# Expert lists' remainders in quarters of 32 slots, paired loads of weights, and no conditional block

## The chip, the cores and the metric

The kernel runs on one core of a Trainium2 chip. The metric is the device time of one execution in microseconds (us); several executions were timed and one was profiled. TensorE (PE, and PEld for its loads of stationary operands), VectorE (DVE), ScalarE (ACT), GpSimd (POOL) and SyncE (SP, which here issues the large loads) work side by side and wait for each other by semaphores. All data is float32.

## The reference

```python
x = x + xattn(ctx_1024, layernorm(x), fside, ...)       # x: 4 x 1024 x 256, context of 77, 16 heads
h = layernorm(x)                                        # 4096 tokens of 256
probs = softmax(h @ Wr); w, idx = top_k(probs, 2)       # 9 experts, each token goes to two of them
cw[t, idx] = w / sum(w)
hidden = silu(h @ Wg[e]) * (h @ Wu[e])                  # 256 -> 704, for each expert e
x = x + einsum(hidden, Wd[e], cw)                       # 704 -> 256, weighted by cw
```

Each of the 4096 tokens is computed by only its two experts, so there are 8192 entries in nine lists of unknown length.

## The kernel before

**Two stages.** In the first, attention is computed in 32 sub-blocks of 128 tokens and each token is put on the lists of its two experts (an entry is the token's number and its weight). The second runs the experts over the lists. Lists lie in memory (`list_d`); normed tokens lie in `y_d`; the output already holds the residual and the experts' results are added to it there.

**Blocks.** The second stage is a sequence of blocks, written out when the kernel is built, whose experts and list places come from tables computed on the chip (`early_blocks`, `late_blocks`, both on VectorE). A *pair* block takes 256 slots of one expert, a *single* block 128. Six pairs ("early") are placed before all lists are complete; the rest after. There are 26 pairs in all (NPAIR). The lists' remainders go in singles: eleven with 128 slots of one expert ("one") and five with two halves of 64 slots, each half of its own expert ("flex"). The order is pair, single, pair, single and so on, with five pairs at the end. The fifth flex block is the *rare* one: its weights are loaded and its rounds of adding are issued in every execution, but its computation stands in `tc.If(count > 2 * (FLEX - RARE))` (L1679) and runs only where a ninth half is needed. In the profiled execution it did not run.

**One block.** For block j, SP loads the expert's weights (`load`, 2.1 MB: gate and up into `wgu`, down into `wd`; three buffers and four). POOL gathers the block's entries (`tokens`, `ids`) and then the tokens' rows (`inputs`, `yin`, three buffers; two gathers for a pair, one for a single). VectorE turns `yin` into `xT` in 16 steps of 32 lanes (`turning`, L1301). `hidden_pair` (L1328) does six products of 128 features with the weights stationary and the 256 tokens moving; ScalarE and VectorE make `hid` of them. `hidden_one` (L1368) does it for a single, tokens stationary; a flex block issues each product twice, for lanes 0 to 63 with one expert's weights and for lanes 64 to 127 with the other's, and its second weights are in an extra set of buffers (`w2`, `d2`). `hidden_turn` (L1391) transposes a single's result. `down` (L1408) multiplies by `wd`, VectorE weights the result (`co`, L1411).

**Adding.** `adding` (L1443) is an indirect DMA of POOL that adds the 128 rows of `co` to the output. Two rows of one round are never the same token. For a pair, the two halves are declared free of each other. A flex block's two experts may hold the same token, so it is added in two *rounds* (`rounds_of`), each with the lanes of the other half sent out of bounds (`split`, `alone`); a round waits until the round before it, whichever block's, has landed.

**Order.** The order on each engine is written by hand. Iteration j of the loop over blocks does, as each engine sees it: `fetch` (weights of j+2, the second weights of a flex block j+3, rows of j+2, entries of j+4), `hidden` of j with the steps of `turning(j + 1)` laid between VectorE's products (from the third feature group on), `down(j - 1)`, `adding` of j-1, and `hidden_turn(j)` for a single. So POOL's queue holds, in this order: gathers of rows for j+2, gather of entries for j+4, adds of j-1, then the same for the next iteration. While early blocks run, VectorE also makes the late tables, up to twelve small operations between two products (`pump`).

The few lines on which that order rests:

```python
for name, fn, lead in (
    ("weights", weights, LEAD), ("weights_upper", weights_upper, LEAD + 1),
    ("inputs", inputs, LEAD), ("tokens", tokens, LEAD + 2),
):
...
    down(j - 1)
    for r in rounds_of(j - 1):
        adding(*r)
```

Of the kernel before, what the change touches and what calls it, by code (L numbers as in the profile page):

```python
# [8 lines left out]
F32 = mybir.dt.float32  # L9
# [6 lines left out]
P = 128  # L16
# [5 lines left out]
def kernel(  # L22
# [54 lines left out]
    U = P // 2  # L77
    HMAX = (2 * TOK + E * (U - 1)) // U
    NPAIR = -((3 * E - 2 * TOK // U) // 4)
    FLEX = (E + 1) // 2  # L80
    NONE = (HMAX - 4 * NPAIR) // 2 - FLEX

    RARE = 1
    LP = TOK + 3 * P
    ROWS = E * LP + (NONE + 1) * P
# [3 lines left out]
    EARLY = 6  # L89
# [280 lines left out]
    with ExitStack() as kvs:  # L370
# [269 lines left out]
        def wide_iota(name, pattern, shape):  # L640
# [4 lines left out]
        NU = TOK // U  # L645
        steps_i, steps = wide_iota("steps", [[0, E], [U, NU]], [P, E, NU])
        num_i, num = wide_iota("num", [[1, NPAIR], [0, E]], [P, NPAIR, E])
# [3 lines left out]
        lane, lower, upper, lane_half, *nowhere = (  # L651
            tab.tile([P, 1], F32, name=n)
            for n in ("lane", "lo", "up", "lane_half", "nowhere0", "nowhere1")
        )

        def numbers():
            for dst, src in ((steps, steps_i), (num, num_i), (lane, lane_i)):
                nc.vector.tensor_copy(dst, src)
            nc.vector.tensor_scalar(upper, lane, float(U), None, ALU.is_ge)
            nc.vector.tensor_scalar(lower, lane, float(U), None, ALU.is_lt)  # L660
            nc.vector.scalar_tensor_tensor(lane_half, upper, -float(U), lane, ALU.mult, ALU.add)
            for t, half in zip(nowhere, (lower, upper)):
                nc.vector.tensor_scalar(t, half, float(TOK), None, ALU.mult)
# [3 lines left out]
        for name in ("early", "pair", "one", "flex"):  # L667
            sums[name] = [tab.tile([P, PAD + E], F32, name=f"{name}_sum{k}") for k in range(5)]
            for t in sums[name]:
                nc.gpsimd.memset(t[:, :PAD], 0.0)  # L670
# [377 lines left out]
    def place(name, src, n, step, size, shift=None, halves=False):  # L1048

        v = nc.vector
        cur = sums[name][0]
        yield v.tensor_copy(cur[:, PAD:], src)
        for k in range(4):
            nxt = sums[name][k + 1]
            yield v.tensor_tensor(
                nxt[:, PAD:], cur[:, PAD:], cur[:, PAD - (1 << k) : PAD + E - (1 << k)], ALU.add
            )
            cur = nxt  # L1060
        ends = tabs[f"{name}_ends"] = cur[:, PAD:]
        past = tab.tile([P, n, E], F32, name=f"{name}_past")
        yield v.tensor_tensor(
            past, num[:, :n, :], ends.unsqueeze(1).to_broadcast([P, n, E]), ALU.is_ge
# [9 lines left out]
        if shift is None:  # L1074
            yield v.tensor_scalar(weight, src, -float(step), float(size), ALU.mult, ALU.add)
        else:
            yield v.tensor_tensor(weight[:, : E - 1], shift[:, 1:], shift[:, : E - 1], ALU.subtract)
            yield v.tensor_scalar(weight[:, E - 1 :], shift[:, E - 1 :], -1.0, None, ALU.mult)
            yield v.tensor_tensor(weight, weight, src, ALU.subtract)
            yield v.tensor_scalar(weight, weight, float(step), float(size), ALU.mult, ALU.add)  # L1080
# [4 lines left out]
        if shift is None:  # L1085
            yield v.tensor_scalar(at, at, lane[:, 0:1], None, ALU.add)
        else:
            first = tab.tile([P, 1], F32, name=f"{name}_first")
            yield v.scalar_tensor_tensor(
                first, shift[:, 0:1], float(step), lane_half if halves else lane, ALU.mult, ALU.add  # L1090
            )
            yield v.tensor_scalar(at, at, first[:, 0:1], None, ALU.add)
        if halves:
            two = at.rearrange("p (m h) -> p m h", h=2)
            n //= 2
            at = tab.tile([P, n], F32, name=f"{name}_both")
            yield v.tensor_scalar(at, two[:, :, 1], upper, None, ALU.mult)
            yield v.scalar_tensor_tensor(at, two[:, :, 0], lower, at, ALU.mult, ALU.add)
        ai = tab.tile([P, n], I32, name=f"{name}_ai")
        yield v.tensor_copy(ai, at)  # L1100
        tabs[name] = (ei, ai)

# [8 lines left out]
    by_pair, by_unit = "p e (k t) -> p e k t", "p e (k t) -> p e k t"  # L1111

    def early_blocks():

        v = nc.vector
        yield from count_of("early")
        full = row("full")
        ends = steps.rearrange(by_pair, t=4)[:, :, 1:, 0]
        begun = tab.tile(list(ends.shape), F32, name="early_begun")
        yield v.tensor_tensor(  # L1120
            begun, ends, tabs["early_count"].unsqueeze(2).to_broadcast(list(ends.shape)), ALU.is_le
        )
        yield v.tensor_reduce(full, begun, AX.X, ALU.add)
        yield from place("early", full, EARLY, P, LP // 2)
        yield from within("early", full, EARLY, taken)

    def late_blocks():
# [3 lines left out]
        rows = {n: row(n) for n in ("pairs", "used", "units", "alone", "halves")}  # L1131
        pairs, used, units, alone, half = rows.values()

        begun = steps
        yield v.tensor_tensor(
            begun, steps, tabs["late_count"].unsqueeze(2).to_broadcast([P, E, NU]), ALU.is_lt
        )
        yield v.tensor_reduce(pairs, begun.rearrange(by_pair, t=4)[:, :, :, 3], AX.X, ALU.add)
        yield v.tensor_tensor(pairs, pairs, taken, ALU.subtract)
        yield from place("pair", pairs, NPAIR - EARLY, P, LP // 2, taken)  # L1140
        yield from within("pair", pairs, NPAIR - EARLY, used)
        yield v.tensor_tensor(used, used, taken, ALU.add)
        yield v.tensor_scalar(used, used, 2.0, None, ALU.mult)
        yield v.tensor_reduce(units, begun.rearrange(by_unit, t=2)[:, :, :, 1], AX.X, ALU.add)
        yield v.tensor_tensor(units, units, used, ALU.subtract)
        yield from place("one", units, NONE, P, LP, used)
        yield from within("one", units, NONE, alone)
        yield v.tensor_tensor(used, used, alone, ALU.add)
        yield v.tensor_scalar(used, used, 2.0, None, ALU.mult)
        yield v.tensor_reduce(half, begun, AX.X, ALU.add)  # L1150
        yield v.tensor_tensor(half, half, used, ALU.subtract)
        yield from place("flex", half, 2 * FLEX, U, LP, used, halves=True)
        total = tab.tile([P, 1], I32, name="flex_total")
        yield v.tensor_copy(total, tabs["flex_ends"][:, E - 1 : E])
        tabs["flex_total"] = total
# [9 lines left out]
    LAST_PAIRS = NPAIR - EARLY - (NONE + FLEX - RARE)  # L1165
    blocks = [(2, i, "early") for i in range(EARLY)]
    made = {"one": 0, "flex": 0}
    for i in range(NPAIR - EARLY):
        blocks.append((2, i, "pair"))
        if i < NPAIR - EARLY - LAST_PAIRS:  # L1170
            kind = "flex" if i % 3 == 1 and made["flex"] < FLEX - RARE else "one"
            blocks.append((1, made[kind], kind))
            made[kind] += 1
    assert made == {"one": NONE, "flex": FLEX - RARE} and RARE == 1 and LAST_PAIRS > 3
    NBLK = len(blocks)
    blocks.append((1, FLEX - RARE, "flex"))
# [5 lines left out]
    def of(tiles, j):  # L1182

        return tiles[j % len(tiles)] if j < NBLK else late[id(tiles)]

    def open_late():
# [3 lines left out]
        for key, shape, name in (  # L1190
            ("w2", [P, C, 2 * FF], "w2"), ("d2", [P, NF + 1, D], "d2"),
            (id(hids), [P, NF + 1, P], "hid_r"), (id(wds), [P, NF + 1, D], "wd_r"),
            (id(yins), [P, 1, D], "yin_r"),
            ("w", [P, C, 2 * FF], "w_r"), ("xT", [P, C, P], "xT_r"), ("co", [P, 1, D], "co_r"),
            ("hs", [P, FF], "hs_r"),
        ):
            late[key] = pool.tile(shape, F32, name=name)

        for t in (late["d2"], late[id(wds)]):
            nc.gpsimd.memset(t[0:64, NF, :], 0.0)  # L1200
        for key in (id(yins), "co"):
            nc.gpsimd.memset(late[key], 0.0)
# [17 lines left out]

    def weights(j, in_parts=False):

        _, i, kind = blocks[j]
        w = late["w"] if j >= NBLK else pools["wpool"].tile(
            [P, C, 2 * FF], F32, tag="wgu", name=f"wgu{j}"
        )
        two = kind == "flex"
        wgus[j] = (w, late["w2"]) if two else (w,)
        downs[j] = (of(wds, j), late["d2"]) if two else (of(wds, j),)
        at = 2 * i if two else i  # L1230
        parts = load(tabs[kind][0][0:1, at : at + 1], w, downs[j][0])
# [5 lines left out]
    def weights_upper(j):  # L1237

        _, i, kind = blocks[j]
        if kind == "flex":  # L1240
            advance(load(tabs[kind][0][0:1, 2 * i + 1 : 2 * i + 2], late["w2"], late["d2"]))
# [48 lines left out]
    def turned_tile(j):  # L1290
        xT = xTs[j] = late["xT"] if j >= NBLK else pools["spool"].tile(
            [P, C, TS], F32, tag="xT", name=f"xT{j}"
# [433 lines left out]
```

## Time and profile before

| | us |
|---|---|
| nine runs: median (lowest to highest) | 878.71 (876.34 to 884.21) |
| the profiled execution's own time | 876.93 |
| its span, first to last instruction | 874.9 |
| PE busy in the span | 860.8 |
| VectorE, POOL busy | 590.1, 313.9 |
| mean granted TensorE clock | 0.997 |

The profiled execution's time is 2.0 us more than its span. All profile figures below are of this one execution, and times within it count from the span's start. PE's matmul records come in two passes for each float32 product, so a product appears as two records. A timeline line gives start, length, engine, source line, operation, what it writes and reads, the count merged into the line, and in brackets the idle time before it and what ended that. The first stage ends and the late blocks begin at about 442 us.

### The profile page before, as it was taken

The page shows a single profiled execution, that of the slowest core. Times are in us where ns is not written, and L with a number is a line of the kernel's source. Part 1 is how long each engine was busy: PE and PEld are TensorE (multiplying, and loading weights), DVE is VectorE, ACT ScalarE, POOL GpSimd, SP SyncE. Part 2 cuts the span into 40 slices and gives each one's busy share as a digit, 9 for nine tenths or more (in the row PEclk, how much of TensorE's full clock was granted, in tenths as well). Part 3 has the DMA queues.
Part 4 walks back from the last instruction along what each step waited for, and adds up shares of the span by engine and source line. Part 5 has one row for each costly group of instructions (what it writes and reads, how often), then busy time and mean ns, then how long its engine had stood idle before and what let it go on. Part 6 is the DMA issues. An engine that isn't in the chain of part 4 may idle for free. (4 is left out here: it accounts for less than half of the span.)

```text
span 874.9 us, 13839 instructions
## 1 busy us (share of the span) xinstructions
PE 860.8 (98%) x3876; PEld 678.6 (78%) x3876; DVE 590.1 (67%) x1807; ACT 354.4 (41%) x1499; POOL 313.9 (36%) x327
## 2 busy tenths in 40 slices
PE   9999999999999999999999999999999999999996
PEld 6755877778778778988887787777777777778885
DVE  5767779998899987546446566666666666664641
ACT  3868687877878686231211111111111111111110
POOL 3000000413404500657574454445426435444332
PEclk9999999999999999999999999999999999999998
DMA  8026656766576785996697797789779778779722
GB/s 277 2 103 178 177 168 198 195 201 171 176 199 169 215 257 172 283 277 192 153 311 205 219 294 238 231 270 293 235 221 323 218 214 228 223 225 315 211 25 25
DMA packets 133005, 181.22 MB, mean 207 GB/s; under 512 B 26999, under 2 KB 98175, under 8 KB 132800
## 3 DMA queue, kind: packets, MB, share of 16 engines
q1 hardware_dynamic: 115306, 162.90, 61.2%
q0 software_dynamic: 17408, 17.29, 10.2%
q8 instruction: 32, 0.52, 0.2%
q14 instruction: 45, 0.37, 0.1%
q10 hardware_dynamic: 214, 0.13, 0.0%
HBM read 141.54 MB, written 40.41 MB: 208 GB/s over the span
## 5 line engine op out<-in xcount | busy, mean ns | idle before, releaser
L1328 PE MATMUL pg<-xT,wgu 128*128 128x256 f32 x1144 | 252.7, 379 | 1.6 <-DMA wd_r<-in_L_ffn_Wd_dram 1.5
L1328 PEld LDWEIGHTS pg<-xT,wgu 128*128 128x128 f32 x1144 | 215.7, 190 | 31.0 <-issue 1.9
L289 ACT ACTIVATE ex<-psc,mx 128x77 f32<-128x77 f32 x512 | 158.8, 331 | 65.2 <-DVE mx L278 64.9
L1408 PE MATMUL po<-wd,hid 128*128 128x256 f32 (+1 forms) x804 | 180.8, 380 | 0.0
L1408 PEld LDWEIGHTS po<-wd,hid 128*128 128x128 f32 (+1 forms) x804 | 149.2, 187 | 28.0 <-issue 3.7
L1301 DVE STREAM_TRANSPOSE xT<-yin 32x128 f32<-32x128 f32 (+1 forms) x544 | 148.4, 273 | 15.4 <-DMA yin<-y_d,ids 7.2
L1016 POOL DMA_INDIRECT list_d<-r_entry,r_pli x64 | 66.3, 1036 | 252.0 <-DVE r_pli L1003 122.0
L350 PE MATMUL po<-u,aT 128*128 128x265 f32 x640 | 155.6, 398 | 0.0
L1443 POOL DMA_INDIRECT out_dram<-co,ids x63 | 100.4, 1594 | 151.3 <-DVE co L1411 124.0
L350 PEld LDWEIGHTS po<-u,aT 128*128 128x128 f32 x640 | 148.7, 312 | 0.5 <-ACT zT L263 0.4
L274 PE MATMUL psc<-g,zT 128*128 128x462 f32 (+1 forms) x384 | 141.4, 513 | 0.6 <-ACT zT L263 0.5
L1334 ACT ACTIVATE sl<-pg 128x256 f32<-128x256 f32 x130 | 49.8, 384 | 226.0 <-PE pg L1328 201.8
L1335 DVE TENSOR_TENSOR hid<-pg,sl 128x256 f32<-128x256 f32 x130 | 55.0, 424 | 125.0 <-ACT sl L1334 124.3
L274 PEld LDWEIGHTS psc<-g,zT 128*128 128x128 f32 x384 | 72.0, 190 | 57.9 <-issue 44.8
L289 ACT ACTIVATION_READ_ACCUMULATOR ex<-psc,mx 128x1 f32 x512 | 107.8, 211 | 0.0
L1266 POOL DMA_INDIRECT yin<-y_d,ids x67 | 70.6, 1053 | 27.2 <-issue 18.5
L330 DVE STREAM_TRANSPOSE anT<-an 128x1280 f32<-128x1280 f32 x32 | 79.7, 2490 | 0.4 <-DMA a_d<-anT 0.4
L278 DVE TENSOR_REDUCE mx<-psc 128x6 f32<-128x462 f32 (+1 forms) x96 | 53.5, 557 | 21.8 <-PE psc L274 21.8
L1411 DVE TENSOR_SCALAR co<-po,ids 128x256 f32<-128x256 f32 x67 | 32.2, 483 | 49.2 <-PE po L1408 47.4
L311 DVE TENSOR_TENSOR an<-ex,rs 128x1024 f32<-128x1024 f32 x32 | 39.2, 1225 | 1.1
L1396 ACT COPY hid<-ph 128x384 f32<-128x384 f32 x15 | 7.2, 479 | 78.4 <-PE ph L1391 78.4
L1372 ACT ACTIVATE hs<-psg 128x512 f32<-128x512 f32 x15 | 9.0, 597 | 65.3 <-PE psg L1368 65.3
(312 smaller groups left out, 762.3 us busy)
## 6 DMA issues: line engine op xcount, KB each, us to landing
wgu<-in_L_ffn_Wg_dram SPq DMA_DIRECT2D x41, 704.0 KB
wd<-in_L_ffn_Wd_dram SPq DMA_DIRECT2D x41, 640.0 KB
wgu<-in_L_ffn_Wu_dram SPq DMA_DIRECT2D x41, 512.0 KB
a_d<-anT SPq DMA_DIRECT2D x32, 640.0 KB
aT<-a_d SPq DMA_DIRECT2D x128, 160.0 KB
wgu<-in_L_ffn_Wu_dram SPq DMA_DIRECT2D x41, 128.0 KB
x<-in_x_dram SPq DMA_DIRECT2D x8, 512.0 KB
out_dram<-x SPq DMA_DIRECT2D x8, 512.0 KB
```

The costliest lines, as they stand in the source:

```text
L274: nc.tensor.matmul(psc[:, :w], zT[:, c, :], g_sb[i // NS // GPB][:, c, h * J : h * J + w], start=(c == 0), stop=(c == C - 1),)
L278: nc.vector.tensor_reduce(nmx[i][:, h : h + n], psc[:, : n * J].rearrange("p (h j) -> p h j", h=n), AX.X, ALU.max, negate=True,)
L289: nc.scalar.activation(exs[i][:, h + q, :], pscs[k][:, q * J : (q + 1) * J], AF.Exp, bias=nmx[i][:, h + q : h + q + 1], accum_out=sms[i][: ...
L330: nc.vector.transpose(turned.rearrange("p q t k -> p q k t"), an_of[0].rearrange("p (k q t) -> p q k t", q=NQ, t=Q))
L350: nc.tensor.matmul(po[:, :DE], aT[:, :, n], u_sb[b][:, n, :], start=(n == 0), stop=(n == KC - 1))
L1016: i = nc.gpsimd.indirect_dma_start(out=list_d[:, :], out_offset=bass.IndirectOffsetOnAxis(ap=place_i[:, s : s + 1], axis=0), in_=entry.bit ...
L1266: return nc.gpsimd.indirect_dma_start(out=dst, out_offset=None, in_=src, in_offset=bass.IndirectOffsetOnAxis(ap=offsets, axis=0), **kw,)
L1301: yield nc.vector.transpose(xT[q : q + Q].rearrange("p c (h t) -> p h c t", t=P)[:, :nh, :, a : a + Q], of(yins, j)[a : a + Q].rearrange(" ...
L1328: nc.tensor.matmul(pg[:, g, :], w[:, c, at : at + P], xT[:, c, :], start=(c == 0), stop=(c == C - 1),)
L1335: made = nc.vector.tensor_tensor(hid[:, f, :], pg[:, 1, :], sl, ALU.mult)
L1408: nc.tensor.matmul(po[rows, :D], hid[:, f, at], d[:, f, :], start=(f == 0), stop=(f == NF))
L1443: i = nc.gpsimd.indirect_dma_start(out=out_r, out_offset=bass.IndirectOffsetOnAxis(ap=rows_of(j, h, rows), axis=0), in_=cos[j][:, h, :], i ...
```

## The change

The lists' remainders are rounded up to quarters of 32 slots, not to halves of 64. The 26 pairs stay. The singles are now seven "one" blocks, five flex blocks, all computed always, and two "quart" blocks: four quarters of 32 slots, each with its own expert, 14 singles where there were 15 computed ones and the rare one. The `tc.If` and what belonged to it are gone.

Twelve of the pairs form six "quads": two pair blocks of the same expert (`quad`, `quad2`) that share one load of weights. A flex block loads one second set of weights, a quart block three; there are three extra sets (`SETS`), loaded up to five blocks ahead. The last block's weights go to one of these sets.

A quart block issues each product of `hidden_one` and `down` four times, with 32 lanes stationary, and adds in four rounds. The order of the late blocks, numbered from 6 (Q quad and quad2, P pair, O one, F flex, X quart):

```text
QO PF PO QX PO QF PF PO QX PO QF PF, then quad, one, quad2, one, pair
quart blocks: 15 and 27; last block: 39
```

The late tables are made by arithmetic on the counts (`whole`, rounding by adding and subtracting a large number) where a compare of 576 steps was; there are more tables (`quad`, `quart`), and 148 VectorE operations from the late counts to the last table where there were 80. The first two late blocks may be fetched as soon as the quads' table is there (`FETCH`).

```diff
-    U = P // 2
...
-    RARE = 1
+    V = P // 4
...
+    NPAIR, EARLY, QUADS, ONES, FLEX, QUART = 26, 6, 6, 7, 5, 2
+    PARTS = {"early": 1, "quad": 1, "quad2": 1, "pair": 1, "one": 1, "flex": 2, "quart": 4}
...
+    def whole(dst, src, n, up=False):
+        frac = (n - 1) / (2 * n)
+        yield nc.vector.tensor_scalar(dst, src, 1 / n, frac if up else -frac, ALU.mult, ALU.add)
+        yield nc.vector.tensor_scalar(dst, dst, NEAREST, -NEAREST, ALU.add, ALU.add)
...
+        yield from place("quad", doubles, QUADS, 2 * P, LP // 2, begin)
+        yield FETCH
...
+        yield from place("quart", rest, 4 * QUART, V, LP, begin)
...
+    SETS = 3
+    order = "QO PF PO QX PO QF PF PO QX PO QF PF"
...
     def weights(j, in_parts=False):
         _, i, kind = blocks[j]
+        if kind == "quad2":
+            wgus[j], downs[j] = quads.pop(i)
+            return
...
+    def weights_upper(k):
+        def begin(j):
+            _, i, kind = blocks[j]
+            sets = uppers.get(j, ()) if j < LAST else ()
+            if k <= len(sets):
+                at = PARTS[kind] * i + len(sets) - k + 1
+                n = sets[-k]
+                advance(load(tabs[kind][0][0:1, at : at + 1], late["w", n], late["d", n]))
...
     def rounds_of(j):
-        n = 2 if blocks[j][2] == "flex" else 1
-        return [(j, rows) for rows in lanes(range(n))]
+        return [(j, rows) for rows in lanes(range(PARTS[blocks[j][2]]))]
...
+    UPPER = [(f"upper{k}", weights_upper(k), LEAD + k) for k in range(1, SETS + 1)]
...
-        if j == RARE_AT:
-            split(NBLK)
-            with tc.If(count > 2 * (FLEX - RARE)):
-                turn(NBLK)
-                hidden_one(NBLK)
-                hidden_turn(NBLK)
-                down(NBLK)
-            rare = rounds_of(NBLK)
-        elif j > RARE_AT and rare:
-            adding(*rare.pop(0))
```

## The prediction

> **What bounds the kernel now.** I read the page's busy shares first, then PE's timeline block by block, then POOL's timeline and waits.
>
> ```profile
> PE 860.8 (98%) x3876; PEld 678.6 (78%) x3876; DVE 590.1 (67%) x1807; ACT 354.4 (41%) x1499; POOL 313.9 (36%) x327
> ...
> 1.47 4.61 PE L165 MATMUL warm<-u 128*128 128x256 f32 x10 [1.47 <-DVE u L161]
> 6.22 1.56 PE L165 MATMUL warm<-u 128*128 128x256 f32 x6
> ...
> 513.21 9.66 PE L1328 MATMUL pg<-xT,wgu 128*128 128x256 f32 x44
> 522.71 2.75 PE L1408 MATMUL po<-wd,hid 128*128 128x256 f32 x12
> 525.49 1.95 PE L1368 MATMUL psg<-wgu,xT 128*128 128x512 f32 x4
> ...
> 530.29 5.34 PE L1408 MATMUL po<-wd,hid 128*128 128x256 f32 x24
> 535.47 0.82 PE L1391 MATMUL ph<-ident,hs 128*128 128x128 f32 x6
> 536.12 9.66 PE L1328 MATMUL pg<-xT,wgu 128*128 128x256 f32 x44
> ...
> 798.26 2.75 PE L1408 MATMUL po<-wd,hid 128*128 128x256 f32 x12
> 802.55 9.73 PE L1328 MATMUL pg<-xT,wgu 128*128 128x256 f32 x44 [1.53 <-DMA wd_r<-in_L_ffn_Wd_dram]
> ...
> 817.30 9.66 PE L1328 MATMUL pg<-xT,wgu 128*128 128x256 f32 x44
> ```
>
> PE works for 860.8 of 874.9 us, and in the late blocks without a hole but one: 1.53 us at 801, where the conditional stands. So PE's own work sets the end, and whatever stops PE is paid in full. A pair and a single take 536.12 - 513.21 = 22.91 us; a pair alone takes 831.98 - 817.30 = 14.68 (the next pair starts at 831.98); a single is worth 8.23.
>
> POOL is busy for 36%, but its queue is in order and its adds wait:
>
> ```profile
> POOL out_dram L1443 <- DMA out_dram<-co,alone: 25.7, 6, 6.0
> ...
> 503.46 1.62 POOL L1443 DMA_INDIRECT out_dram<-co,alone  x1 [7.37 <-DVE co L1411]
> 511.06 1.59 POOL L1443 DMA_INDIRECT out_dram<-co,alone  x1 [5.98 <-DMA out_dram<-co,alone]
> 512.95 1.07 POOL L1266 DMA_INDIRECT yin<-y_d,ids  x1 [0.30 <-issue]
> 514.33 1.01 POOL L1266 DMA_INDIRECT ids<-list_d,flex_ai  x1 [0.30 <-issue]
> 517.55 1.62 POOL L1443 DMA_INDIRECT out_dram<-co,ids  x1 [2.21 <-DMA out_dram<-co,alone]
> ...
> 837.52 2.71 DMA out_dram<-co_r,alone
> ...
> L740 PE MATMUL pwl<-woT,wc x16: 379/379/403, 41.5 to 42.2; 128*32 128x256 f32 x16
> ```
>
> A flex block's second round starts 7.60 us after its first, released by the first one's landing, and the rows of a later block (L1266) are gathered only behind it. I take this, and not PE, as what decides the change. The line at 837.52 is of the chain of waits: a round with every row out of bounds, 2.71 us from issue to landing on quiet DMAs.
>
> **The change, part by part.** All against the profiled execution: 876.93 us, span 874.9.
>
> *One single less.* 15 computed singles become 14: -8.23 on PE.
>
> *No conditional.* The hole of 1.53 goes. A part of it is the turning of xT, which ended at 801.48 (VectorE's last group, 800.22 + 1.26) where PE was free at 801.0: that is a pair behind a pair with only a single's down between. Two such places come (blocks 14 and 26), each at least 0.5, and their gathers stand behind a flex block's two rounds: 0.5 to 2.0 each, I take 1.0. Together -1.53 + 2.0 = +0.5.
>
> *Flex and quart on PE.* Periods with a flex block take 23.04 and 22.99 against 22.91: 0.2 per flex block. One flex more, and two quarts at 0.2 to 0.4: +0.8 at most. That four products with 32 lanes run side by side is in the L740 line: 16 records of 256 columns start within 0.7 us, where the 128-lane records above take 5.18 / 24 = 0.216 each, so four share a slot. If they ran in turn, a quart's products, 4.7 + 2.6 us, would take three times as much more: +44 us for two.
>
> *Late tables.* 148 operations where there were 80. Before, VectorE was at it from 400 to 420 and 86% busy (18.94 of the 22 us from 399); 68 more at 0.21 are 14 us and end at about 435. From 424 VectorE was nearly idle (3.52 of 16 us from 426), and PE needs the new blocks at 442. Five PSUM banks let PE run 8 us ahead, and by twelve operations (2.5) and one product (0.4) per 1.73 us of PE the lag stays under that. Nothing on the path; if the cover failed, up to 7.
>
> *Weights.* 47 loads become 45. By 7.3 us a load (2.1 MB at the 290 GB/s of busy stretches) and the buffers' releases, each late load lands 12 us or more before its block. Nothing; the extra loads of a quart are spread over three iterations. The first late loads start earlier (DMA share was 0.39 from 400 to 411).
>
> *Four rounds of a quart.* This is where a wait is added. Let T be PE's start on the pair behind quart 15 (block 16). As behind a flex block (490.22 to 503.46) the first round is issued at T + 13.24. Each further round waits for the landing of the one before. Behind the fourth in POOL's queue stand the two gathers of rows for block 19, the entries of 21, the adds of 16. With S the sum of the three spacings, the second gather is issued at T + 13.24 + S + 1.9 + 1.4, and lands 5.1 later (median; 2.7 to 8.4). Then VectorE, whose queue stands at the first of these 16 steps in the middle of block 18, has to do four groups of 1.25 and three products of 0.43: 6.3. So xT of block 19 is there at T + S + 27.9. PE reaches block 19 at T + 12.33 + 10.66 + 9.5 + 2.7 = T + 35.2. PE stands still for S - 7.2 us. Block 31 behind quart 27 is the same.
>
> The spacing: behind rounds with rows, the flex blocks show 7.60, 6.66, 7.59, 6.68, 6.49 and 5.74 (mean 6.8, 64 rows, DMA share 0.85 to 1.0). Behind a round without rows: 3.0 (2.71 + 0.3, quiet) to 4.8 (716.96 to 721.73). The routing of the given inputs fills five of the eight quarters: all four of block 15, one of block 27. A round of 32 rows may land sooner than one of 64: between 3.9 and 6.8, I take 6.1, nearer to the row with rows. Quart 15: S = 18.3, stall 11.1. Quart 27: S = 6.1 + 3.9 + 3.9 = 13.9, stall 6.7. Together +17.8. At the shortest (3.0 all) S = 9.0 and 1.8 each, 3.6 in all; at the longest (7.6, 4.8) 15.6 + 10.0 = 25.6.
>
> In its section on the anatomy of one DMA on the GpSimd path, the Trainium skill's page "DMA: Bandwidth & Descriptors" puts it at about 2.0 us and bytes / 436e3. By it a round of 32 KB would be an estimated 2.1, behind 1.6 of issue and 0.3: spacing 4.0, stalls of 4.8 each and a total of 879, no change. The rows of the trace are far above that beside loads, so I go by them.
>
> *PE after standing.* Records at the start, after idling, are spaced 0.46 (4.61 / 10) and soon 0.22: 2.3 us lost. After the hole of 1.53 nothing (9.73 against 9.66). Between 0 and 2.3 for each stall; idle for 7 to 11 us is nearer to the start: 2.0 each, +4.0. The granted clock reads 1.00 in all of these, so that row doesn't tell it. By Part 1 (the HAM clock gate) of the Trainium skill's page "TensorE: Matmul & The Clock Gate" the array falls to half speed after 3.4 us of idling and needs as long to recover, an estimated 1.7 per stall.
>
> *The end.* Last down, two adds, landing: as before.
>
> Sum: -8.23 + 0.5 + 0.8 + 17.8 + 4.0 = +14.9: 891.8. The nine runs' median lies 1.8 above the profiled execution; I give 892. Bounds: -8.23 - 0.5 + 0.2 + 3.6 = -4.9, 872; and -8.23 + 2.5 + 0.8 + 25.6 + 4.6 = +25.3, 902.
>
> **Rivals.** (1) *The rounds are short enough*: with S under 7.2 there is no stall, and PE's gain stands: -8.23 + 0.5 + 0.8 = -6.9, 870, faster; with some stall 870 to 872. From S = 10.7 at both quarts (spacing 3.6) the gain is gone. For it: a round without rows lands in 2.71, and block 27 has three such. Against it: every spacing behind a round with rows is 5.7 or more. 0.14. (2) *Rounds of about 3.6 us*, as the byte count would have it: stalls of 3 to 5 each, 874 to 881, no change. 0.07. (3) *The 32-lane products run in turn*: 892 + 44 = 936. The L740 line speaks against it. 0.02. (4) *Longer landings or a further late chain*, as loads held back during a stall crowd the next block: over 903. 0.07. (5) *The change doesn't do what it says*: the single less and the four rounds are in the order of instructions, so only the quads' saving of loads could be void, and that is off the path anyway: nothing.
>
> **How the numbers follow.** Measurement of this kernel tells about 0.5% (4.4 us) from no change. Forecast (stalls of 12 to 27 in all, 881 to 903): 0.70, 892. With (3) and (4) slower is 0.79; same 0.07; faster 0.14. The range 875 to 903 leaves out (1) and the parts of (3) and (4) over it, about 0.2.
>
> **What would show it.** In the profile after: PE idle before L1402 at two places, released by VectorE's xT steps and those by the gather of yin; POOL waiting for DMA out_dram<-co,alone six times more, by 4 us or more behind filled rounds; the larger stall at the first quart; 14 ph groups, not 15; 0.21 per 32-lane slot. It is wrong if PE has no hole behind the quarts, if spacings of filled rounds are under 4, or if PE waits for weights.

## The result, and the profile after

The kernel after takes 906.0 us (median of 19 runs) where the kernel before takes 877.3 (62 runs): ratio 1.0327, interval 1.0307 to 1.0346. It is slower by some 29 us; 892 was predicted, with a range of 875 to 903, so that 906.0 lies 3 above it. The profiled execution took 903.45 us (span 901.5), to be set against 876.93 (span 874.9): 26.6 us of span are to be explained.

First the page of the kernel after: busy time, the granted clock in 40 slices, and the pairs' product in the list of groups (busy time, mean ns, then the idle time before it and what ended it).

```profile
PE 859.7 (95%) x4014; PEld 673.1 (75%) x4014; DVE 595.4 (66%) x1868; ACT 352.4 (39%) x1496; POOL 316.3 (35%) x340
...
PEclk9999999999999999999999999988999999699999
...
L1402 PE MATMUL pg<-xT,wgu 128*128 128x256 f32 x1100 | 249.1, 386 | 30.7 <-DVE xT L1375 30.6
```

PE is busy for 1.1 us less than before, though one single (8.23) has gone; and it now stands idle for 30.6 us ahead of pairs, always for VectorE's turning of xT. PE's timeline has the five places (start, duration, what, and in brackets the idle time before it and its releaser):

```profile
540.56 9.74 PE L1402 MATMUL pg<-xT,wgu 128*128 128x256 f32 x44 [1.54 <-DVE xT L1375]
...
613.25 11.69 PE L1402 MATMUL pg<-xT,wgu 128*128 128x256 f32 x44 [11.81 <-DVE xT L1375]
...
689.66 9.76 PE L1402 MATMUL pg<-xT,wgu 128*128 128x256 f32 x44 [2.01 <-DVE xT L1375]
...
705.22 11.42 PE L1402 MATMUL pg<-xT,wgu 128*128 128x256 f32 x44 [3.21 <-DVE xT L1375]
...
779.86 12.01 PE L1402 MATMUL pg<-xT,wgu 128*128 128x256 f32 x44 [12.07 <-DVE xT L1375]
```

These are blocks 14, 19, 25, 26 and 31. The large two (19 and 31) come four blocks behind the quarts (15 and 27), where the prediction put them. The holes at 25 and 26 come behind two flex blocks that stand close together (20 and 22). The pairs' products behind three of the holes take 11.42 to 12.01 instead of 9.66: the granted clock is 0.50 for a part of them (windows further down).

What PE waits for is VectorE, VectorE waits for the gathered rows, and the gathers stand in POOL's queue behind the rounds of adds. The waits of the kernel after (us in total, times, longest), then POOL's timeline behind quart 15, then VectorE's:

```profile
POOL out_dram L1518 <- DMA out_dram<-co,alone: 59.9, 11, 6.4
...
DVE xT L1375 <- DMA yin<-y_d,ids: 33.9, 7, 11.5
```

```profile
579.48 1.61 POOL L1518 DMA_INDIRECT out_dram<-co,alone  x1 [7.38 <-DVE co L1481]
585.48 1.57 POOL L1518 DMA_INDIRECT out_dram<-co,alone  x1 [4.39 <-DMA out_dram<-co,alone]
592.88 1.55 POOL L1518 DMA_INDIRECT out_dram<-co,alone  x1 [5.83 <-DMA out_dram<-co,alone]
600.41 1.55 POOL L1518 DMA_INDIRECT out_dram<-co,alone  x1 [5.98 <-DMA out_dram<-co,alone]
602.26 1.07 POOL L1342 DMA_INDIRECT yin<-y_d,ids  x1 [0.30 <-issue]
603.64 1.05 POOL L1342 DMA_INDIRECT yin<-y_d,ids  x1 [0.30 <-issue]
```

```profile
606.64 1.25 DVE L1375 STREAM_TRANSPOSE xT<-yin 32x128 f32<-32x128 f32 x4 [11.22 <-DMA yin<-y_d,ids]
```

The four rounds are 6.00, 7.40 and 7.53 apart, S = 20.93 in all. Only behind them do the two gathers for block 19 go out, and VectorE has stood 11.22 us at the first of its steps when they land. Behind quart 27 it is the same, with 6.57, 7.58 and 7.10 (S = 21.25).

The sum: -8.23 (a single) - 1.53 (the conditional's hole) + 30.64 (five holes) + 6.3 (slow products behind the holes: 2.03, 1.76, 2.35 and 0.2) + 0.8 (flex and quart on PE) + 0.6 (the transposes ahead of block 25, at 686.78, with a short wait and a slow pace) - 0.9 (from PE's last product to the end of the span 7.3, not 8.2) - 1.1 (the late blocks begin at 440.80, not 441.94) = +26.6, against 26.6 measured.

### The profile page after: what moved, and what is told of

The parts are those of the page before. It is cut to its first block, busy times and chain, and to the rows that moved or that the text cites. A ratio compares the mean times of both kernels' runs of the same rounds, so it can differ in the third digit from the quotient of the medians.

```text
span 901.5 us, 14079 instructions
## 1 busy us (share of the span) xinstructions
PE 859.7 (95%) x4014; PEld 673.1 (75%) x4014; DVE 595.4 (66%) x1868; ACT 352.4 (39%) x1496; POOL 316.3 (35%) x340
## 4 chain that ended last, share of the span: by engine, by line
PE 63%; issue 16%; DMA 11%; POOL 5%; DVE 3%; ACT 2%; POOLq 0%; DVEq 0%
PE po L354 17%; PE pg L1402 14%; PE psc L278 14%; PE po L1478 9%; DMA out_dram<-co,ids 7%; POOL out_dram L1518 3%; DMA out_dram<-co,alone 2%; DMA yin<-y_d,ids 1%; PE psg L1440 1%; PE psu L1440 1%; POOL yin L1342 1%; PE pv L777 1%; PE psb L1440 1%; PE warm L169 1%; PE pgk L703 1%
## 5 line engine op out<-in xcount | busy, mean ns | idle before, releaser
L1402 PE MATMUL pg<-xT,wgu 128*128 128x256 f32 x1100 | 249.1, 386 | 30.7 <-DVE xT L1375 30.6
L1402 PEld LDWEIGHTS pg<-xT,wgu 128*128 128x128 f32 x1100 | 211.4, 194 | 61.9 <-issue 30.1
L1478 PE MATMUL po<-wd,hid 128*128 128x256 f32 (+2 forms) x768 | 173.2, 381 | 0.0
L1375 DVE STREAM_TRANSPOSE xT<-yin 32x128 f32<-32x128 f32 (+1 forms) x528 | 144.6, 274 | 41.9 <-DMA yin<-y_d,ids 33.9
L1478 PEld LDWEIGHTS po<-wd,hid 128*128 128x128 f32 (+2 forms) x768 | 139.3, 183 | 30.4 <-issue 3.8
L1518 POOL DMA_INDIRECT out_dram<-co,ids x59 | 94.1, 1596 | 145.9 <-DVE co L1481 111.6
L1518 POOL DMA_INDIRECT out_dram<-co,alone x18 | 28.6, 1587 | 99.8 <-DMA out_dram<-co,alone 59.9
L1481 DVE TENSOR_SCALAR co<-po,ids 128x256 f32<-128x256 f32 x66 | 31.6, 483 | 44.2 <-PE po L1478 43.1
```

The source lines that it names most:

```text
L1375: yield nc.vector.transpose(xT[q : q + Q].rearrange("p c (h t) -> p h c t", t=P)[:, :nh, :, a : a + Q], of(yins, j)[a : a + Q].rearrange(" ...
L1402: nc.tensor.matmul(pg[:, g, :], w[:, c, at : at + P], xT[:, c, :], start=(c == 0), stop=(c == C - 1),)
L1478: nc.tensor.matmul(po[rows, :D], hid[:, f, at], d[:, f, :], start=(f == 0), stop=(f == NF))
L1518: i = nc.gpsimd.indirect_dma_start(out=out_r, out_offset=bass.IndirectOffsetOnAxis(ap=rows_of(j, h, rows), axis=0), in_=cos[j][:, h, :], i ...
```

## The experiments

**Theories.** A: PE has its gain; all of the loss is that serial rounds on POOL stand ahead of gathers that are needed soon, and the slow clock behind the holes. Rivals: the loss is PE's or the weights' (32-lane products, four loads for a quart, sharing in quads); or an add delays something else than gathers. And within A a question that decides the size: is a round's landing set by its rows, as the prediction had it, or by what else the DMAs carry?

Two things help to read the times. Beside the first four experiments the kernel before took 898.7 us, and in their traces the late blocks begin at 464 to 465 us and not at 441; why is not known. Beside e9 and e10 it took 877.9 and beside the others 880.5, but some executions there lose up to 11 us as well before the late blocks begin. So beside the ratio I give the **late span**: from the first late pair's product of gate and up (L1402; L1328 in the kernel before) to the end of the span. It is 874.9 - 441.94 = 433.0 in the kernel before and 901.5 - 440.80 = 460.7 after.

**The rounds of a quart, spread** (e1_spread_quarts). The buffers of co go from 3 to 5, so that co lives until the last round.

```diff
...
         fetch()
+        if owed:
+            adding(*owed.pop(0))
...
-            for r in rounds_of(j - 1):
-                adding(*r)
+            first, *more = rounds_of(j - 1)
+            adding(*first)
+            if blocks[j - 1][2] in ("quart",):
+                owed.extend(more)
+            else:
+                for r in more:
+                    adding(*r)
```

> Rounds 2 to 4 of a quart are issued one per later block, each right behind that block's gathers, not all four in a row ahead of them. Theory (the serial rounds stand ahead of the gathers of rows, PE's own saving is intact): the stalls of 11.81 and 12.07 us and the 4 us of slow clock behind them go, 906 - 28 = 878 us, while the smaller holes of 1.5 to 3.2 behind blocks 13, 24 and 25, which come from flex blocks, stay. Rival (the loss is PE's: 32-lane products, or loads of a quart's four weights): the holes stay where they are and the time stays above 900.

900.0 us, ratio to the kernel before 1.0026 (0.9986 to 1.0066). The absolute 878 cannot be set against it, where the kernel before takes 898.7; the ratio agrees with it, and the late span is 901.1 - 465.02 = 436.1, 24.6 less than after, where 28 was expected. At blocks 19 and 31 0.61 is left of 11.81 and 12.07:

```profile
628.34 9.73 PE L1402 MATMUL pg<-xT,wgu 128*128 128x256 f32 x44 [0.61 <-DVE xT L1375]
...
781.73 9.73 PE L1402 MATMUL pg<-xT,wgu 128*128 128x256 f32 x44 [0.61 <-DVE xT L1375]
```

At 14, 25 and 26 stay 1.92, 2.01 and 3.25, and the product behind 14 is now slow as well (11.42 for 9.74), which with its larger hole is over half of what is short of 28. The rounds in a row were the cause of the two large holes, and the quart's products and loads were not, since they are untouched. That co has two buffers more here could be a second cause; e5 below keeps three, and the holes go there too.

**All rounds spread** (e2_spread_all): the same with `in ("quart", "flex")`.

> As e1_spread_quarts, and the second round of a flex block goes one block later too. Theory: the holes at blocks 25 and 26 (2.01 and 3.21, with 1.8 of slow clock) go as well, 878 - 6 = about 871 (868 to 874), faster than the kernel before (877.3), since only the single less, the conditional's hole and at most 2 us of small holes are left. Rival (those holes come from weights or from VectorE's own work): they stay, and the time is that of e1_spread_quarts. Second rival (an add put behind a later block's gathers delays that block's own adds and so the buffers): new holes, over 878.

895.7 us, ratio 0.9962 (0.9934 to 0.999), where the expected 871 would be 0.993; late span 895.1 - 464.43 = 430.7. The hole at 26 falls to 0.61, that at 14 as well; at 25 the 2.01 stays, with 11.45 for the product behind it. So half of the expectation on the flex blocks failed: a round that is put off one block is only moved, and its landing still held an add at 681.72 back for 9.57 us and with it the gathers behind that add:

```profile
672.15 1.61 POOL L1518 DMA_INDIRECT out_dram<-co,alone  x1 [4.19 <-DMA out_dram<-co,alone]
681.72 1.58 POOL L1518 DMA_INDIRECT out_dram<-co,ids  x1 [7.96 <-DVE hid L1409]
...
685.46 1.07 POOL L1342 DMA_INDIRECT yin<-y_d,ids  x1 [0.31 <-issue]
```

The line names VectorE, which had written that co (L1481) by 673.5; that it was the landing of the round at 672.15 I infer, as the add may not start before that.

**Empty rounds** (e3_empty_rounds): nothing of a quart is added.

```diff
-                alone[j][:, k : k + 1], ids[j][:, 0, 0:1], nowhere[n][:, k : k + 1], None, ALU.add
+                alone[j][:, k : k + 1], ids[j][:, 0, 0:1],
+                float(TOK) if n == 4 else nowhere[n][:, k : k + 1], None, ALU.add,
```

> All four rounds of both quarts have every row out of bounds, so nothing of a quart is added to the output; the instructions and the loads are as in the kernel after. Theory (what a round waits for is set by the weight loads that occupy the DMAs, not by its rows): spacings stay at 6.0 to 7.6 us at both quarts, both holes stay at 11 to 12, 903 to 906. Rival (a round without rows lands early, 2.7 as on quiet DMAs, which is what the prediction priced): spacings 3.0 to 4.0, S of 9 to 12, holes of 2 to 5 each, 882 to 890.

The rounds of quart 15, every row out of bounds, in POOL's timeline, from the second on (the first starts at 604.10):

```profile
610.02 1.57 POOL L1519 DMA_INDIRECT out_dram<-co,alone  x1 [4.31 <-DMA out_dram<-co,alone]
617.35 1.55 POOL L1519 DMA_INDIRECT out_dram<-co,alone  x1 [5.76 <-DMA out_dram<-co,alone]
624.59 1.55 POOL L1519 DMA_INDIRECT out_dram<-co,alone  x1 [5.70 <-DMA out_dram<-co,alone]
```

5.92, 7.33 and 7.24 apart, and 6.31, 7.39 and 7.15 behind quart 27; the holes are 11.37 and 11.68, the late span 459.9. (The time of its one execution, 927.0, was expected at 903 to 906; the kernel before took 898.7 beside it, so only the late span can be compared.) A round without a single row lands as late as a full one: the rows are not what it waits for.

**Quiet DMAs** (e4_quiet_loads): blocks 17 to 20 and 29 to 32 compute with the weights of blocks 16 and 28 and load none of their own.

```diff
...
+        if j in (17, 18, 19, 20, 29, 30, 31, 32):
+            two = PARTS[kind]
+            wgus[j], downs[j] = kept["w"][:1] * two, kept["d"][:1] * two
+            return
...
+            if k <= len(sets) and j not in (20, 32):
```

> Blocks 17 to 20 and 29 to 32 load no weights of their own (a flex block's second set neither), but use those of blocks 16 and 28 again, so their outputs are computed with other experts' weights; the rounds carry the same rows as in the kernel after. The loads of blocks 21 and 22 can start early and may still lie beside the first round or two. Theory (loads set the landing): the rounds that lie beside no loads are 3.0 to 4.5 apart, rows or none, S falls from 21 to 12 to 16, holes to 5 to 9. Rival (rows or a fixed price of an add): 6.0 to 7.6 apart as before, holes of 11 to 12.

Two windows around quart 15's rounds (length, busy us and instructions of PE, PEld, DVE, ACT and POOL, granted clock, DMA share, GB/s), and the rounds from the second on (the first starts at 603.95):

```profile
604.00:611.00 7.00, 7.00 (x26) 4.67 (x25) 5.22 (x17) 0.93 (x2) 1.58 (x2) 1.00 0.93 310
611.00:619.00 8.00, 8.00 (x41) 7.07 (x41) 2.69 (x7) 1.25 (x3) 3.37 (x3) 1.00 0.32 93
```

```profile
610.97 1.57 POOL L1523 DMA_INDIRECT out_dram<-co,alone  x1 [5.42 <-DMA out_dram<-co,alone]
615.29 1.55 POOL L1523 DMA_INDIRECT out_dram<-co,alone  x1 [2.75 <-DMA out_dram<-co,alone]
618.72 1.55 POOL L1523 DMA_INDIRECT out_dram<-co,alone  x1 [1.88 <-DMA out_dram<-co,alone]
```

The first spacing lies beside loads and takes 7.02; then the loads end, and the same 32 rows follow at 4.32 and 3.43. The windows of the three spacings themselves have DMA shares of 0.93, 0.55 and 0.07. Behind quart 27 it goes 6.32, 5.09, 3.01, at 0.93, 0.64 and 0.02. The holes fall to 5.67 and 5.25, the late span to 446.8 (914.2 us for its one execution). Together with e3: the weight loads that occupy the DMAs set the spacing.

**Three rounds in a row, the fourth put off** (e10_three_in_a_row), with five buffers of co as in e1.

```diff
...
+            rounds = rounds_of(j - 1)
+            for r in rounds[:3]:
+                adding(*r)
+            owed.extend(rounds[3:])
```

> Three rounds of a quart are issued in a row, the fourth one block later, behind that block's gathers. Theory (PE's hole is the sum S of the spacings ahead of the gathers less a constant; the kernel after and e4_quiet_loads give 20.9, 14.8 -> 11.81, 5.67, so the constant is 9.1): S of 13.4 to 14.2, holes of 4 to 5.5 at blocks 19 and 31, with 2 us of slow clock behind each. Rival (a hole comes with the fourth round, or with the quart's four loads, not with the sum): no hole, or 11 to 12 as in the kernel after.

The holes are 8.04 and 8.52: neither the theory's 4 to 5.5 nor what the rival asks. S was about as expected (14.00 and 14.31, for 13.4 to 14.2), so the constant was wrong. It had been taken from runs in which the gather behind the rounds found quiet DMAs and landed in 3.0 (DMA share 0.21 from 602 to 607 us in the kernel after); here it lay beside loads (0.92), from 607.09 to 613.26:

```profile
607.09 1.05 POOL L1342 DMA_INDIRECT yin<-y_d,ids  x1 [0.30 <-issue]
...
613.26 1.25 DVE L1375 STREAM_TRANSPOSE xT<-yin 32x128 f32<-32x128 f32 x4 [7.46 <-DMA yin<-y_d,ids]
...
619.87 12.56 PE L1402 MATMUL pg<-xT,wgu 128*128 128x256 f32 x44 [8.04 <-DVE xT L1375]
```

The slow clock behind the holes took 2.9 and 2.6 there, not 2; the late span is 455.1 (908.5 us for its one execution). With S for the time from the first round to the last and L for the time from the issue of the last gather to VectorE's first turn, all ten places come under one line:

| kernel, quart | S | L | hole | S + L - hole |
|---|---|---|---|---|
| after, 15 and 27 | 20.93, 21.25 | 3.00, 2.95 | 11.81, 12.07 | 12.12, 12.13 |
| after again (e8) | 20.80, 21.54 | 2.99, 2.99 | 11.67, 12.40 | 12.12, 12.13 |
| e3, empty | 20.49, 20.85 | 3.00, 2.96 | 11.37, 11.68 | 12.12, 12.13 |
| e4, quiet | 14.77, 14.42 | 3.00, 2.98 | 5.67, 5.25 | 12.10, 12.15 |
| e10, three | 14.00, 14.31 | 6.17, 6.34 | 8.04, 8.52 | 12.13, 12.13 |

The hole is S + L - 12.1, to 0.05 us. The 12.1 is PE's work in between, less what else POOL and VectorE have to do. In the kernel after, behind quart 15, PE reaches block 19 35.23 after it starts on block 16 (566.21); from there the chain takes 13.27 to the first round, then, beside S and L, 3.23 from the last round to the last gather and 6.61 for the turning, and 35.23 - 13.27 - 3.23 - 6.61 is 12.12. That it is the same in ten places says that only S and L change among them.

**The gathers one block earlier** (e5_gather_earlier), the rounds and the three buffers of co left as in the kernel after. The slot of yin that block j + 3 takes is that of block j, turned before PE begins on j, so no buffer is added.

```diff
+        far = 1 if late else 0
...
-            ("inputs", inputs, LEAD), ("tokens", tokens, LEAD + 2),
+            ("inputs", inputs, LEAD + far), ("tokens", tokens, LEAD + 2 + far),
...
-                while ahead["tokens"] < min(now[0] + LEAD + 1, end):
+                while ahead["tokens"] < min(now[0] + LEAD + far + 1, end):
```

> The four rounds of a quart and the two of a flex block stay one behind the other as in the kernel after; only the gathers of rows and of list entries of the late blocks are issued one block earlier, so ahead of the rounds (the buffer of the rows is free by then). Theory (a round costs only because gathers that are needed soon stand behind it): with one block of 12 to 15 us more room, S - 7.2 - 15 is below nothing, the holes at blocks 14, 19, 25, 26 and 31 go, 28 to 34 us below the kernel after and 5 to 7 below the kernel before (ratio 0.992 to 0.995). At most the 0.61 per pair behind a pair that e1 and e2 show stays. Rival (the landing of rounds delays something else too, buffers of co or the DMAs): holes of several us stay, over 1.005.

870.2 us, ratio 0.9896 (0.9831 to 0.9961), somewhat more than expected; the interval holds the expected 0.992 to 0.995. The same kernel, with more executions:

> The same kernel as e5_gather_earlier, with more rounds beside the kernel before. Theory: ratio 0.988 to 0.995, the late blocks take 425 to 427 us from the first pair's L1402 to the end of the span (e5: 425.7; the kernel before: 433.0). Rival (e5's gain was chance): 0.998 or more.

870.9 us against 877.9, ratio 0.9893 (0.985 to 0.9936), late span 869.0 - 443.33 = 425.7 as in e5, which is 35.0 less than after. Its page, waits, and POOL around the rounds of quart 15:

```profile
PE 853.8 (98%) x4014; PEld 668.9 (77%) x4014; DVE 595.5 (69%) x1868; ACT 353.1 (41%) x1496; POOL 316.8 (36%) x340
```

```profile
POOL out_dram L1518 <- DMA out_dram<-co,alone: 63.4, 13, 6.8
...
PE pg L1402 <- DVE xT L1375: 2.4, 4, 0.6
```

```profile
571.37 1.06 POOL L1342 DMA_INDIRECT yin<-y_d,ids  x1 [0.30 <-issue]
...
602.05 1.55 POOL L1518 DMA_INDIRECT out_dram<-co,alone  x1 [6.05 <-DMA out_dram<-co,alone]
```

POOL waits for landings no less than in the kernel after (63.4 us to 59.9), and the rounds are as far apart (5.87, 7.51 and 7.60). But block 19's gathers now go out at 570 and 571, ahead of them, and of PE's 30.6 us of holes 2.4 are left, 0.61 at each pair that follows a pair with only a down between. This is the proof of A by its other end: the waiting is there, and costs nothing once no near gather stands behind it. It is also some 1% shorter than the kernel before: the interval leaves out 1, but the gain is under 2%.

**Both together** (e6_both: e5 and e2 in one).

> e2_spread_all and e5_gather_earlier together. Theory: nothing is left for the second to take, so the same as e5_gather_earlier within 0.3%; against e2_spread_all, the hole of 2.01 at block 25 and the 1.8 of slow clock behind it go. Ratio to the kernel before 0.990 to 0.994. Rival (e2's remaining hole is VectorE's own work): ratio 0.996 as e2.

Late span 875.9 - 450.14 = 425.8, the same as e5: the second has nothing left to take. The time is 876.8, ratio 0.9929 (0.9896 to 0.9963); its profiled execution had lost 6 us before the late blocks, ahead of block 6. The eleven executions fall into two groups, four at 870.7 to 871.8 and seven at 875.3 to 878.4, so the median lies 0.75% above e5's, though the late spans agree.

**Quads without sharing** (e7_unshared: e6 with `if kind == "quad2": ... return` taken out, so that the second pair of a quad loads its weights too).

> e6_both, but the second pair of each quad loads its weights itself: 51 late loads for 45. Prediction's term for the sharing was nothing, as loads land 12 us or more before their block: then the same as e6_both within 0.3%, with the DMAs busier and the rounds somewhat later. Rival (the loads fill the DMAs: 6 x 7.3 = 44 us more in a stretch that is 0.75 busy): PE waits for wgu, 5 to 20 us more.

Late span 878.2 - 452.75 = 425.5, again the same, which decides here; the time is 869.7 (four executions at 868.6 to 870.2, two at 880), ratio 0.9856 (0.9808 to 0.9904). Six more loads raise the DMA share from 0.85 to 0.96 (470 to 640 us) and from 0.74 to 0.85 (640 to 860), and PE does not wait for one of them. The sharing brings nothing that these runs can tell.

**The kernel after again** (e8_after_again), beside these four.

> The kernel after, unchanged, beside the others on one chip: 1.030 to 1.035 of the kernel before, with holes at blocks 14, 19, 25, 26 and 31 within 0.5 us of the first trace's 1.54, 11.81, 2.01, 3.21 and 12.07.

913.0 us, ratio 1.0344 (1.0293 to 1.0396); late span 911.2 - 451.42 = 459.8. The holes are 2.08, 11.67, 2.01, 1.72 and 12.40: the large ones repeat, the small ones less well (the fourth is 1.5 smaller than in the first trace).

## Why the prediction was right, and where it was wrong

**Right.** Which wait decides (the rounds ahead of the gathers), where PE would stand (blocks 19 and 31, and pairs behind a pair), and the sign. PE's own terms: -8.23 + 0.5 + 0.8 with no stalls is -6.9, and where the rounds are out of the way (e5, e9) the late span is 7.3 below that of before. That the two agree is in part luck: 0.9 of the 7.3 is a shorter end (7.3 from PE's last product to the end of the span, where it was 8.2), which the prediction had "as before". The first quart's stall: 11.1 predicted, 11.81 measured. Its rival 3, that 32-lane products run in turn, is out: the quart's three products start at 555.41 and its successor at 560.27, 4.86 for the 4.72 to 4.83 of a single. The quads' loads: nothing, as e7 shows.

**The first quart was right by two errors that cancel.** S was put at 18.3 and was 20.93; the landing of the gather was put at 5.1, from the median, and was 3.0, since by then the loads had run ahead and stopped. The prediction's own numbers, 35.2 - 27.9 + 5.1, make its constant 12.3 for the measured 12.1: the chain of steps was sound, and the two durations put into it were not. The sign that was named for this, a larger stall at the first quart than at the second, came the other way round: 11.81 and 12.07.

**Wrong, the term for rounds without rows.** This is the step that failed by most: a round's landing was priced by its rows. For quart 27 the prediction took 6.1 + 3.9 + 3.9, as three of its four quarters are empty, a spacing of 3.9 for such a round, with 3.0 and 4.8 for the bounds. Measured were 6.57, 7.58 and 7.10, and the hole was 12.07 for 6.7. The row of 2.71 that set the low bound was of the end of the kernel, on quiet DMAs; the loads beside the rounds should have been read from it, not the rows in the round. The rows that were taken for "a round with rows" were in truth rows beside loads. The price by the Trainium skill, "DMA: Bandwidth & Descriptors", its section on the anatomy of one DMA on the GpSimd path (an estimated spacing of 4.0), lies above e4's two rounds on quiet DMAs (3.43 and 3.01, shares 0.07 and 0.02) and below all that lie beside loads (5.87 to 7.60).

**Wrong, the places behind flex blocks.** One us each at 14 and 26 was taken, 2.0 in all. There were three places, 14, 25 and 26, with 1.54 + 2.01 + 3.21 = 6.76, and with them 0.6 for the transposes ahead of block 25. What seems to lie behind 25 and 26 is that two flex blocks (20 and 22) come so close that the second's rounds queue up behind what the first's have delayed:

```profile
662.22 1.57 POOL L1518 DMA_INDIRECT out_dram<-co,alone  x1 [6.39 <-DMA out_dram<-co,alone]
664.09 1.07 POOL L1342 DMA_INDIRECT yin<-y_d,ids  x1 [0.30 <-issue]
...
689.27 1.58 POOL L1518 DMA_INDIRECT out_dram<-co,alone  x1 [5.96 <-DMA out_dram<-co,alone]
...
692.53 1.05 POOL L1342 DMA_INDIRECT yin<-y_d,ids  x1 [0.30 <-issue]
```

That it is this queue I infer from its order. Flex blocks 32 and 34 stand as close and leave no hole; their rounds are 6.76 and 3.97 apart. What the runs do show is that the places go too when the gathers go out a block earlier (e5, e9). The prediction had followed one block at a time, not POOL's queue over three.

**The clock.** 2.0 for each of two stalls was predicted; 2.03 and 2.35 came, and 1.76 more behind the hole of 3.21, which was not foreseen. That it is the granted clock shows in the windows after the first large hole, the first of them starting with PE's product:

```profile
613.00:616.00 3.00, 2.75 (x7) 2.24 (x8) 0.59 (x2) 0.00 (x0) 1.79 (x2) 0.50 0.01 0
616.00:618.00 2.00, 2.00 (x8) 1.65 (x7) 0.42 (x1) 0.38 (x1) 1.69 (x2) 0.70 0.75 107
618.00:624.00 6.00, 6.00 (x30) 5.28 (x29) 2.82 (x10) 1.15 (x3) 1.16 (x2) 1.00 0.11 30
```

The reading of the prediction that the profile does not tell it was true of the kernel before, which has no such hole. The traces tell more than the lengths of the holes. In all of them the granted clock is 1.00 or 0.50, and within a trace it changes only at points that lie a whole number of 3.41 us apart. In the kernel after it is 0.50 from 603.57 to 617.22 (four times 3.41), around the first large hole, and from 705.97 to 709.38 (once), behind the hole of 3.21:

```profile
702.56:705.97 3.41, 0.75 (x4) 0.70 (x5) 2.87 (x9) 0.00 (x0) 1.12 (x3) 1.00 0.18 29
705.97:709.38 3.41, 3.41 (x10) 2.65 (x9) 0.42 (x1) 0.39 (x1) 2.80 (x3) 0.50 0.32 38
709.38:712.80 3.42, 3.42 (x17) 3.02 (x16) 0.45 (x2) 0.77 (x2) 1.73 (x2) 1.00 0.30 82
```

From 430 us on, in every trace of this case, each such stretch at 1.00 in which PE was busy for 0.44 of the time or less (here 0.75 of 3.41 us) is followed by one at 0.50, and none in which it was busy for 0.49 or more. So where a hole lies on this grid decides as well as how long it is. The estimate of 1.7 per stall from Part 1 of "TensorE: Matmul & The Clock Gate" in the Trainium skill is near 1.76 to 2.35. The prediction read the page's idle window as 3.4 us of standing still, and that was not needed here: in e10 the clock fell behind a hole of 1.91, after a stretch of 3.41 us in which PE was busy for 0.44 of the time.

**The sum.** Of the 11.7 us between 14.9 predicted and 26.6 found, 5.4 are quart 27's stall, 0.7 quart 15's, 4.8 the places behind flex blocks, 0.6 the transposes ahead of block 25 and 2.3 the clock (6.3 for 4.0); the earlier start of the late blocks takes 1.1 off and the shorter end 0.9. The range's upper end added the term of each bound for itself; its 4.8 for an empty round and 2.0 per small place were both too low at once. Its bounds hold nothing for the distance of a median from a profiled execution: 903.45, the profiled time, is above 903 by only 0.45, and the median by 3.

**Open.** The kernel after's median lies 2.5 above its profiled execution, and that of before only 0.4. Several executions lose 6 to 8 us ahead of block 6, where PE waits for the first late rows (6.1 in e6, 8.4 in e7, 6.3 in e8, 7.3 in e10; the traces of before and after do not show it). The entries of block 6 seem to wait there for the landing of the last places of the lists. Why it comes in some executions and not in others, and whether the change makes it more frequent, was not tried; nor was why e1 to e4 begin their late blocks some 24 us later.

## What to carry to other kernels

An operation that must wait for a landing costs what stands behind it in its queue, not what it moves: before adding one, walk that queue to the next thing that someone needs soon, and if buffers allow issue that first. Price a small DMA by the row that lies beside the same traffic, not by the row that moves the same bytes. Two right answers from one sum are no test of its parts: measure each duration that goes into it where it will lie.

## What the runs showed that was not expected

An add with every row out of bounds lands no sooner than one with 32 or 64 rows: 5.92 to 7.39 beside loads (DMA share 1.04 and 1.05), while 32 rows on quiet DMAs (share 0.07) take 3.43. The granted clock falls to half (0.50) at every hole of 3.21 us or more; around 2 us it goes either way, by where the hole lies on the grid of 3.41 us: behind 2.01 the product takes 9.76 in the kernel after, 11.45 in e8 and e2.
